# Group-normalisation statistics: two-operand steps on VectorE or on GpSimd

## The chip, the cores and the metric

The kernel runs on one core of one Trainium2 chip. The number that counts is the device time of one execution in microseconds (us). Before the change it is 6019.81 us, the median of three runs from 6017.21 to 6021.95. A profile of one execution, with a span of 6018.0 us, stands behind every other number here. The engines are called by the profile's names: PE is TensorE (matmuls), PEld its weight loads, DVE is VectorE, ACT is ScalarE, POOL is GpSimd, SP is the queue that issues transfers.

## The reference

Two layers on an input of 16 images, 56 x 56 pixels, 384 channels, in float32. Each layer normalises by groups and adds its result to its input.

```python
def _gn(v, G=32, eps=1e-5):                      # 32 groups of 12 channels, statistics per image
    g = v.reshape(B_, H_, W_, G, C_ // G)
    m = jnp.mean(g, axis=(1, 2, 4), keepdims=True)
    s = jnp.var(g, axis=(1, 2, 4), keepdims=True)
    return ((g - m) / jnp.sqrt(s + eps)).reshape(v.shape)

# layer 0: attention over 3x3 neighbours, three groups of channels with dilations 1, 2, 3
x = x + _L0_conv_ref(_gn(x), L0_conv_w_qkv, L0_conv_w_proj, L0_conv_b_proj)
# layer 1: depthwise 3x3 convolution with the signs of the weights
x = x + _L1_conv_ref(_gn(x), L1_conv_w)
```

So there are 32 group normalisations in all, two for each image. Each needs the whole image before it can give a mean and an inverse deviation, and everything behind it in its layer needs those.

## The kernel before

Channels lie on the partitions (three tiles of 128). An image is worked on in seven chunks of eight rows (448 pixels). Three stages are planned side by side: stage A turns the input round and gathers statistics of the first normalisation, stage B is the attention, stage C the convolution. Every piece of work is filed under a time slice, nine slices to a chunk, and the slices of different chunks and stages lie over each other:

```python
def at(when, order, piece):
    pieces.setdefault((when, order), []).append(piece)
...
SOFTMAX, SCORE, STATISTICS, CONVOLVE, WEIGH, QUERY, QKV, PROJECT, STAGE_A, STAGE_C, NORM, LOADS = range(12)
STEP = 9
for m in range(N):                 # N = 16 images x 7 chunks
    plan_a(m, STEP * (m - 9))
    plan_b(m, STEP * m)
    plan_c(m, STEP * (m + 10))
for key in sorted(pieces):
    for piece in pieces[key]:
        piece()
```

The recorded pieces are then put into an order for each engine by a scheduler; each engine executes its own row in that order. The heavy work of a chunk, cut to what is spoken of later:

```python
# score(i): query times keys, nine times a chunk
nc.vector.tensor_tensor(t..., q3, k3, ALU.mult)                       # L452, q3 in PSUM, k3 in SBUF
# ... then matmuls of t with sel add up the heads: ps (L437)

# softmax_2, softmax_3
nc.vector.tensor_tensor(by_neighbour(weights), by_neighbour(weights), over_neighbours(sm), ALU.mult)   # L485
nc.scalar.copy(term[0], e8)
nc.gpsimd.tensor_tensor(r8, e8, term[0], ALU.subtract)                # rest, L495
nc.scalar.copy(term[1], r8)
nc.gpsimd.tensor_tensor(term[2], r8, term[1], ALU.subtract)           # e, L497

# weigh(i): weights spread by a matmul (pb_a, L515), times values, summed; nine times a chunk
nc.vector.tensor_tensor(w..., pb[...], three(kv[1][g][m % V_SLOTS], DIL[g], ky), ALU.mult)   # L521, pb in PSUM
...
nc.gpsimd.tensor_tensor(w0, w0, w, ALU.add)                           # L529
if ky == 2:
    nc.gpsimd.tensor_tensor(y, w0[:, 0], w0[:, 1], ALU.add)           # L532
    nc.gpsimd.tensor_tensor(y, y, w0[:, 2], ALU.add)                  # L533
```

The statistics themselves are five pieces for each normalisation. Sums over the 12 channels of a group, and the way back from groups to channels, go through matmuls with 0/1 matrices (`gsel`, `gselT`); the inverse root is found by three Newton steps from an integer guess:

```python
def group_norm(stats, done):
    def channels():                                   # slice 0
        ... nc.vector.bn_aggr(ch[:, j, :], ...)       # mean and variance of each channel
    def mean():                                       # slice 1
        ... matmuls pm                                # L289
        nc.vector.tensor_scalar_mul(pair[:, 2:3], pm[:GN_G, 0:1], 1.0 / GN_CH)        # L292
    def deviation():                                  # slice 2
        ... matmuls pb                                # L299
        nc.vector.tensor_sub(dev, ch[:, :, 0], pb[:, :NG])                            # L301
        nc.vector.tensor_mul(dev, dev, dev)                                           # L302
        nc.vector.tensor_add(dev, dev, ch[:, :, 1])                                   # L303
    def invert():                                     # slice 3
        ... matmuls pv                                # L309
        nc.vector.tensor_scalar(v, pv[:GN_G, 0:1], 1.0 / GN_CH, 1e-5, ...)            # L312
        nc.vector.tensor_single_scalar(ri, v.bitcast(I32), 1, op=ALU.arith_shift_right)   # L315
        nc.vector.tensor_scalar(ri, ri, -1, RSQRT_BITS, op0=ALU.mult, op1=ALU.add)    # L316
        for step in range(3):
            nc.vector.scalar_tensor_tensor(t, r, v, r, op0=ALU.mult, op1=ALU.mult)    # L318
            nc.vector.tensor_scalar(t, t, -0.5, 1.5, op0=ALU.mult, op1=ALU.add)       # L319
            nc.vector.tensor_mul(pair[:, 1:2] if step == 2 else r, r, t)              # L320
        nc.vector.scalar_tensor_tensor(pair[:, 0:1], pair[:, 2:3], -1.0, pair[:, 1:2], ...)   # L321
    def spread_out():                                 # slice 4
        ... matmuls pp                                # L328
        nc.vector.tensor_copy(mr..., pp[:, : 2 * NG]) # L332
        done(mr)
    return channels, mean, deviation, invert, spread_out
```

`dev` has 128 partitions and three columns, everything from `v` on 32 partitions and one column. ScalarE normalises later with `mr` (bias and scale of `Identity`: L398 for the first layer, L624 and L666 for the second).

Of the kernel before, what the change touches and what calls it, by code (L numbers as in the profile page):

```python
# [8 lines left out]
F32 = mybir.dt.float32  # L9
# [3 lines left out]
ALU = mybir.AluOpType  # L13
# [7 lines left out]
NG = 3  # L21
# [4 lines left out]
GN_CH = 12  # L26
GN_G = 32
# [8 lines left out]
def dilated_attention_then_binary_conv(  # L36
# [28 lines left out]
    nc = tc.nc  # L65
# [10 lines left out]
    def place(p):  # L76

        g, o = divmod(p, NTAP)
        return NG * o + g
# [27 lines left out]
    for p in range(NG * NTAP):  # L107
        v = place(p)
# [126 lines left out]
    st_p = ctx.enter_context(tc.tile_pool(name="st_p", bufs=2))  # L235
# [3 lines left out]
    for which, slots in enumerate((K_SLOTS, V_SLOTS)):  # L239
        kv.append([])  # L240
        for g, d in enumerate(DIL):
            kv[which].append([])
            for s in range(slots):
                t = const.tile([P, ROWS + 2 * d, W + 2 * d], F32, name=f"{'kv'[which]}_{g}_{s}")
# [11 lines left out]
    for s in range(2):  # L256
        t = const.tile([P, ROWS + 2, W + 2], F32, name=f"zg_{s}")
# [17 lines left out]

    def group_norm(stats, done):

        had = {}

        def channels():  # L280
            had["ch"] = ch = st_p.tile([P, NG, 2], F32, tag="ch", name="ch")
            for j in range(NG):
                nc.vector.bn_aggr(ch[:, j, :], stats[:, j].rearrange("p c s -> p (c s)"))

        def mean():
            had["pair"] = pair = st_p.tile([GN_G, 3], F32, tag="pair", name="pair")
            pm = ps_mt.tile([P, 512], F32, tag="mt", name="pm")
            for j in range(NG):
                nc.tensor.matmul(  # L289
                    pm[:GN_G, 0:1], gsel[:, j], had["ch"][:, j, 0:1], start=(j == 0), stop=(j == NG - 1)  # L290
                )
            nc.vector.tensor_scalar_mul(pair[:, 2:3], pm[:GN_G, 0:1], 1.0 / GN_CH)  # L292

        def deviation():

            ch = had["ch"]
            pb = ps_mt.tile([P, 512], F32, tag="mt", name="pb")
            for j in range(NG):
                nc.tensor.matmul(pb[:, j : j + 1], gselT[:, j], had["pair"][:, 2:3], start=True, stop=True)  # L299
            had["dev"] = dev = st_p.tile([P, NG], F32, tag="dev", name="dev")  # L300
            nc.vector.tensor_sub(dev, ch[:, :, 0], pb[:, :NG])  # L301
            nc.vector.tensor_mul(dev, dev, dev)  # L302
            nc.vector.tensor_add(dev, dev, ch[:, :, 1])  # L303

        def invert():
            dev, pair = had["dev"], had["pair"]
            pv = ps_mt.tile([P, 512], F32, tag="mt", name="pv")
            for j in range(NG):
                nc.tensor.matmul(pv[:GN_G, 0:1], gsel[:, j], dev[:, j : j + 1], start=(j == 0), stop=(j == NG - 1))  # L309
            var = st_p.tile([GN_G, 3], F32, tag="var", name="var")  # L310
            v, r, t = var[:, 0:1], var[:, 1:2], var[:, 2:3]
            nc.vector.tensor_scalar(v, pv[:GN_G, 0:1], 1.0 / GN_CH, 1e-5, op0=ALU.mult, op1=ALU.add)  # L312

            ri = r.bitcast(I32)
            nc.vector.tensor_single_scalar(ri, v.bitcast(I32), 1, op=ALU.arith_shift_right)  # L315
            nc.vector.tensor_scalar(ri, ri, -1, RSQRT_BITS, op0=ALU.mult, op1=ALU.add)  # L316
            for step in range(3):
                nc.vector.scalar_tensor_tensor(t, r, v, r, op0=ALU.mult, op1=ALU.mult)  # L318
                nc.vector.tensor_scalar(t, t, -0.5, 1.5, op0=ALU.mult, op1=ALU.add)  # L319
                nc.vector.tensor_mul(pair[:, 1:2] if step == 2 else r, r, t)  # L320
            nc.vector.scalar_tensor_tensor(  # L321
                pair[:, 0:1], pair[:, 2:3], -1.0, pair[:, 1:2], op0=ALU.mult, op1=ALU.mult
            )

        def spread_out():
            pp = ps_mt.tile([P, 512], F32, tag="mt", name="pp")
            for j in range(NG):
                nc.tensor.matmul(  # L328
                    pp[:, 2 * j : 2 * j + 2], gselT[:, j], had["pair"][:, 0:2], start=True, stop=True
                )  # L330
            mr = st_p.tile([P, NG, 2], F32, tag="mr", name="mr", bufs=4)
            nc.vector.tensor_copy(mr.rearrange("p j s -> p (j s)"), pp[:, : 2 * NG])  # L332
            done(mr)

        return channels, mean, deviation, invert, spread_out

    def chunk_of(dram, c):
        return dram.rearrange("(j p) n -> p j n", p=P)[:, :, c * PX : (c + 1) * PX]
# [3 lines left out]
    def at(when, order, piece):  # L342

        pieces.setdefault((when, order), []).append(piece)
# [5 lines left out]
    def plan_a(m, t0):  # L350

        b, c = divmod(m, NCH)
        had = {}

        def load():
            if c == 0:
                stats0[b] = st_p.tile([P, NG, NCH, 6], F32, tag="stats0", name="stats0")
                xd[b] = dr_p.tile([C, H * W], F32, tag="xd", name="xd")
            had["xin"] = xin = xin_p.tile([SUB, NSUB, C], F32, tag="xin", name="xin")
            nc.sync.dma_start(xin, xf[b, c * PX : (c + 1) * PX, :].rearrange("(s p) c -> p s c", p=SUB))  # L360

        def turn(j):
            pt = ps_mt.tile([P, 512], F32, tag="mt", name="pt_x")
            for s in range(NSUB):
                nc.tensor.transpose(
                    pt[:, s * SUB : (s + 1) * SUB], had["xin"][:, s, j * P : (j + 1) * P], ident[:SUB, :SUB]
                )
            xa = xa_p.tile([P, PX], F32, tag="xa", name="xa")
            nc.scalar.copy(xa, pt[:, :PX])
            nc.vector.bn_stats(stats0[b][:, j, c, :], xa)  # L370
            nc.sync.dma_start(xd[b][j * P : (j + 1) * P, c * PX : (c + 1) * PX], xa)

        steps = {}

        def norm(k):
            if k == 0:
                steps["of"] = group_norm(stats0.pop(b), lambda mr: mr0.update({b: mr}))
            steps["of"][k]()

        at(t0 - 3, LOADS, load)  # L380
        for j in range(NG):
            at(t0 + 2 * j, STAGE_A, lambda j=j: turn(j))
        if c == NCH - 1:
            for k in range(5):
                at(t0 + 5 + k, STATISTICS, lambda k=k: norm(k))

    def plan_b(m, t0):

        b, c = divmod(m, NCH)
        had = {}  # L390
# [176 lines left out]
        def norm(k):  # L567
            if k == 0:
                steps["of"] = group_norm(stats1.pop(b), for_convolution)
            steps["of"][k]()  # L570
# [18 lines left out]
        for j in range(NG):  # L589
            at(t0 + 23 + j, PROJECT, lambda j=j: out_project(j))  # L590
        if c == NCH - 1:
            for k in range(5):
                at(t0 + 26 + k, STATISTICS, lambda k=k: norm(k))

    def plan_c(m, t0):
# [121 lines left out]
    for m in range(N):  # L717
# [3 lines that stand above are left out]
# [31 lines left out]
```

## Time and profile before

| engine | busy us | share of the span |
|---|---|---|
| TensorE (PE) | 5493.3 | 91% |
| VectorE (DVE) | 4382.1 | 73% |
| GpSimd (POOL) | 4191.8 | 70% |
| ScalarE (ACT) | 2616.6 | 43% |

A profile gives for every instruction its start and its length, and, from the semaphores, who ended the idle time before it. In a list of waits, "PE ps L437 <- DVE var L319" says that TensorE's instruction on line 437, which writes the tile `ps`, started when VectorE's on line 319, which writes `var`, had ended. A group's line gives how often the instruction runs, and its mean time or its shortest, median and longest. The heaviest groups of VectorE are the products of lines 521 (1556.5 us) and 452 (1543.5 us), those of GpSimd the additions of line 529 (2046.8 us) and, in the convolution, of line 681 (680.6 us). All of them are 128 x 1344 elements. Shares of busy time are averages over the whole span; which engine holds up the others can differ from stretch to stretch, so windows and timelines are read as well.

### The profile page before, as it was taken

Reading aid. Unit: us, or ns where it says so; the run is one execution under the profiler, and the core shown is the slowest. Engines: PE = TensorE matmul, PEld = TensorE weight load, DVE = VectorE, ACT = ScalarE, POOL = GpSimd, SP = SyncE. Lnnn points to the kernel's source line nnn. Section 1 sums busy time; section 2 is a strip of 40 time slices with the busy share of each in tenths; the row PEclk is TensorE's granted clock in tenths of the full one; section 3 lists DMA queues with packets and bytes.
Section 4 is the critical chain, followed back from the end, with each engine's and each line's share of the span. In section 5 each row is a group of like instructions: output and inputs, shape, how many; then the busy total and the mean of one; then the engine's idle time right before and its main releaser. Section 6 shows DMA issues by size and latency. Waiting matters only on the chain. (4 is left out here: it accounts for less than half of the span.)

```text
span 6018.0 us, 79851 instructions
## 1 busy us (share of the span) xinstructions
PE 5493.3 (91%) x28693; PEld 2517.5 (42%) x28693; DVE 4382.1 (73%) x4501; ACT 2616.6 (43%) x4714; POOL 4191.8 (70%) x2596
## 2 busy tenths in 40 slices
PE   5998999999999999999999999999999999999955
PEld 3443444444444444444444444444444444444421
DVE  3777777777777777777777778777777777777740
ACT  2223444544444444444544444444444444444435
POOL 1556677777777777777776777777777876777874
PEclk9998999999999999999999999999999999999975
DMA  4322444544445444444544444454444544433434
GB/s 148 100 90 89 123 134 135 145 134 131 136 130 146 135 132 134 135 130 134 145 139 128 132 132 139 128 146 135 129 136 132 147 135 131 134 118 105 115 99 119
DMA packets 629587, 776.73 MB, mean 129 GB/s; under 512 B 177091, under 2 KB 618950, under 8 KB 629190
## 3 DMA queue, kind: packets, MB, share of 16 engines
q1 hardware_dynamic: 624016, 771.01, 44.4%
q8 instruction: 227, 3.72, 0.3%
q14 instruction: 170, 1.39, 0.1%
q10 hardware_dynamic: 5174, 0.61, 0.1%
HBM read 468.47 MB, written 231.21 MB: 116 GB/s over the span
## 5 line engine op out<-in xcount | busy, mean ns | idle before, releaser
L529 POOL TENSOR_TENSOR w<-w 128x1344 f32<-128x1344 f32 x672 | 2046.8, 3046 | 789.7 <-DVE w L521 701.3
L521 DVE TENSOR_TENSOR w<-pb_a,v 128x1344 f32<-128x1344 f32 x1008 | 1556.5, 1544 | 350.1 <-PE pb_a L515 318.4
L452 DVE TENSOR_TENSOR t<-pq,k 128x1344 f32<-128x1344 f32 x1008 | 1543.5, 1548 | 239.6 <-PE pq L402 237.3
L402 PE MATMUL pkv<-xn,wqkvT 128*128 128x448 f32 x4032 | 1686.9, 569 | 0.0
L402 PEld LDWEIGHTS pkv<-xn,wqkvT 128*128 128x128 f32 x4032 | 771.3, 199 | 773.5 <-issue 708.3
L681 POOL TENSOR_TENSOR m<-m 128x1344 f32<-128x1344 f32 x224 | 680.6, 3039 | 296.9 <-ACT m L675 292.0
L402 PE MATMUL pq<-xn,wqkvT 128*128 128x448 f32 x2016 | 866.2, 564 | 0.0
L437 PE MATMUL ps<-t,sel 128*32 128x448 f32 x6048 | 766.8, 562 | 103.8 <-DVE var L319 62.6
L547 PE MATMUL po<-y,wprojT 128*128 128x448 f32 x2016 | 829.7, 548 | 23.5 <-POOL y L533 23.5
L675 ACT ACTIVATE m<-zg,ktap 128x448 f32<-128x448 f32 x1008 | 591.2, 660 | 426.8 <-POOL m L681 419.9
L641 PE MATMUL pc<-z,kdiag 96*32 96x440 f32 (+1 forms) x5376 | 575.0, 563 | 78.2 <-ACT z L624 42.4
L624 ACT ACTIVATE z<-z,mrz 96x448 f32<-96x448 f32 x896 | 627.5, 760 | 2.4 <-DMA mrz<-mr 2.3
L412 ACT COPY v<-pkv 128x448 f32<-128x448 f32 x336 | 177.9, 529 | 1030.1 <-PE pkv L402 1030.0
L550 DVE SCALAR_TENSOR_TENSOR xr<-po,bias,xr 128x448 f32<-128x448 f32 x336 | 228.6, 680 | 444.9 <-PE po L547 444.8
L547 PEld LDWEIGHTS po<-y,wprojT 128*128 128x128 f32 x2016 | 375.0, 191 | 380.9 <-issue 345.3
L402 PEld LDWEIGHTS pq<-xn,wqkvT 128*128 128x128 f32 x2016 | 357.7, 192 | 360.8 <-issue 360.8
L515 PE MATMUL pb_a<-aT,spread 24*128 24x448 bf16 x3024 | 386.7, 366 | 114.9 <-DVE w L521 110.5
L648 DVE TENSOR_TENSOR x<-pc,x 128x448 f32<-128x448 f32 x224 | 139.6, 623 | 368.8 <-PE pc L641 368.2
L533 POOL TENSOR_TENSOR y<-y,w 128x448 f32<-128x448 f32 x336 | 385.1, 1146 | 19.4
L532 POOL TENSOR_TENSOR y<-w 128x448 f32<-128x448 f32 x336 | 386.7, 1151 | 16.9
L515 PEld LDWEIGHTS <-spread 24*128 24x128 bf16 x3024 | 107.8, 92 | 604.3 <-issue 560.2
L398 ACT ACTIVATE xn<-xn,mr 128x448 f32<-128x448 f32 x336 | 234.5, 753 | 288.7 <-DMA xn<-xd 162.2
(111 smaller groups left out, 4869.6 us busy)
## 6 DMA issues: line engine op xcount, KB each, us to landing
z<-x1d SPq DMA_DIRECT2D x608, 224.0 KB, 3.8
xin<-in_x_dram SPq DMA_DIRECT2D x112, 672.0 KB, 6.4
xd<-xa SPq DMA_DIRECT2D x336, 224.0 KB, 2.2
xn<-xd SPq DMA_DIRECT2D x112, 672.0 KB, 4.4
xr<-xd SPq DMA_DIRECT2D x112, 672.0 KB, 4.1
x1d<-xr SPq DMA_DIRECT2D x112, 672.0 KB, 3.2
out_dram<-osb SPq DMA_DIRECT2D x448, 168.0 KB, 2.3
x<-x1d SPq DMA_DIRECT2D x112, 448.0 KB, 6.9
```

The source lines that it names most:

```text
L402: nc.tensor.matmul(dst[:, :PX], wqkvT[:, cc, o0 : o0 + P], had["xn"][:, cc, :], start=(cc == 0), stop=(cc == NG - 1))
L437: return nc.tensor.matmul(had["ps"][32 * j : 32 * j + 32, :PX], sel[:, s0 : s0 + 32], tk, start=(i == 0), stop=(p + NQ >= NG * NTAP),)
L452: nc.vector.tensor_tensor(t.rearrange("p k (r w) -> p k r w", w=W), q3, k3, ALU.mult)
L515: return nc.tensor.matmul(pb[:, kx, :PX], spread[rows_of, v % 2, :], had[f"a{v // 8}"][rows_of, :], start=True, stop=True)
L521: nc.vector.tensor_tensor(w.rearrange("p k (r w) -> p k r w", w=W), pb[:, :, :PX].rearrange("p k (r w) -> p k r w", w=W), three(kv[1][g][m ...
L529: nc.gpsimd.tensor_tensor(w0, w0, w, ALU.add)
L532: nc.gpsimd.tensor_tensor(y, w0[:, 0], w0[:, 1], ALU.add)
L547: nc.tensor.matmul(po[:, :PX], wprojT[:, g, j * P : (j + 1) * P], had[f"y{g}"], start=(g == 0), stop=(g == NG - 1))
L624: nc.scalar.activation(z[:, q], z[:, q], AF.Identity, bias=mrz[:, j, q, 0:1], scale=mrz[:, j, q, 1:2])
L641: return nc.tensor.matmul(pcr[q * HD : (q + 1) * HD, :, lo:hi], kdiag[:, kx, j * NQ + q, :], rows(z[:, q])[:, :, lo + kx - 1 : hi + kx - 1 ...
L675: nc.scalar.activation(rows(t[:, kx]), zp[:, ky : ky + ROWS, kx : kx + W], AF.Copy, scale=ktap[:, o : o + 1])
L681: nc.gpsimd.tensor_tensor(had["m"], had["m"], t, ALU.add)
```

## The change

Every step of the statistics whose two tensor operands both lie in SBUF goes from VectorE to GpSimd. [...] the steps that read a matmul's result stay on VectorE. The mean is kept with its sign turned, so that the deviation is an addition and the last product needs no extra factor. The fused product of three operands becomes two products. The piece `invert` is cut in two, `variance` (matmul and integer guess, VectorE) and `invert` (Newton steps, GpSimd), so there are six pieces in six slices instead of five in five. It is meant to keep these small steps out of VectorE's row.

```diff
-            nc.vector.tensor_scalar_mul(pair[:, 2:3], pm[:GN_G, 0:1], 1.0 / GN_CH)
+            nc.vector.tensor_scalar_mul(pair[:, 2:3], pm[:GN_G, 0:1], -1.0 / GN_CH)
...
-            nc.vector.tensor_sub(dev, ch[:, :, 0], pb[:, :NG])
-            nc.vector.tensor_mul(dev, dev, dev)
-            nc.vector.tensor_add(dev, dev, ch[:, :, 1])
+            nc.vector.tensor_tensor(dev, pb[:, :NG], ch[:, :, 0], ALU.add)
+            nc.gpsimd.tensor_tensor(dev, dev, dev, ALU.mult)
+            nc.gpsimd.tensor_tensor(dev, dev, ch[:, :, 1], ALU.add)
 
-        def invert():
+        def variance():
...              (matmuls pv, v and the integer guess as before, on VectorE)
+        def invert():
             for step in range(3):
-                nc.vector.scalar_tensor_tensor(t, r, v, r, op0=ALU.mult, op1=ALU.mult)
-                nc.vector.tensor_scalar(t, t, -0.5, 1.5, op0=ALU.mult, op1=ALU.add)
-                nc.vector.tensor_mul(pair[:, 1:2] if step == 2 else r, r, t)
-            nc.vector.scalar_tensor_tensor(
-                pair[:, 0:1], pair[:, 2:3], -1.0, pair[:, 1:2], op0=ALU.mult, op1=ALU.mult
-            )
+                nc.gpsimd.tensor_tensor(t, r, r, ALU.mult)
+                nc.gpsimd.tensor_tensor(t, t, v, ALU.mult)
+                nc.gpsimd.tensor_scalar(t, t, -0.5, 1.5, op0=ALU.mult, op1=ALU.add)
+                nc.gpsimd.tensor_tensor(pair[:, 1:2] if step == 2 else r, r, t, ALU.mult)
+            nc.gpsimd.tensor_tensor(pair[:, 0:1], pair[:, 2:3], pair[:, 1:2], ALU.mult)
...
-        return channels, mean, deviation, invert, spread_out
+        return channels, mean, deviation, variance, invert, spread_out
...              (for both layers)
-            for k in range(5):
+            for k in range(6):
```

In the changed file the lines move by a few numbers: the pair of additions on `dev` is L305 and L306, the Newton steps L326 to L329, the last product L330, `pp` L335, `mr` L339.

More of the change, by code (lines that the diff above doesn't have):

```diff
@@ L300, in deviation @@
             had["dev"] = dev = st_p.tile([P, NG], F32, tag="dev", name="dev")
-            nc.vector.tensor_sub(dev, ch[:, :, 0], pb[:, :NG])
-            nc.vector.tensor_mul(dev, dev, dev)
-            nc.vector.tensor_add(dev, dev, ch[:, :, 1])
-        def invert():
-            dev, pair = had["dev"], had["pair"]
+            nc.vector.tensor_tensor(dev, pb[:, :NG], ch[:, :, 0], ALU.add)
+            nc.gpsimd.tensor_tensor(dev, dev, dev, ALU.mult)
+            nc.gpsimd.tensor_tensor(dev, dev, ch[:, :, 1], ALU.add)
+        def variance():
+            dev = had["dev"]
             pv = ps_mt.tile([P, 512], F32, tag="mt", name="pv")
@@ L309, in invert @@
                 nc.tensor.matmul(pv[:GN_G, 0:1], gsel[:, j], dev[:, j : j + 1], start=(j == 0), stop=(j == NG - 1))
-            var = st_p.tile([GN_G, 3], F32, tag="var", name="var")
-            v, r, t = var[:, 0:1], var[:, 1:2], var[:, 2:3]
+            had["var"] = var = st_p.tile([GN_G, 3], F32, tag="var", name="var")
+            v, r = var[:, 0:1], var[:, 1:2]
             nc.vector.tensor_scalar(v, pv[:GN_G, 0:1], 1.0 / GN_CH, 1e-5, op0=ALU.mult, op1=ALU.add)
@@ L316, in invert @@
             nc.vector.tensor_scalar(ri, ri, -1, RSQRT_BITS, op0=ALU.mult, op1=ALU.add)
+        def invert():
+            var, pair = had["var"], had["pair"]
+            v, r, t = var[:, 0:1], var[:, 1:2], var[:, 2:3]
             for step in range(3):
[L318 to L321, printed above, removed]
-                pair[:, 0:1], pair[:, 2:3], -1.0, pair[:, 1:2], op0=ALU.mult, op1=ALU.mult
-            )
+                nc.gpsimd.tensor_tensor(t, r, r, ALU.mult)
[3 more added lines that the diff above has]
+            nc.gpsimd.tensor_tensor(pair[:, 0:1], pair[:, 2:3], pair[:, 1:2], ALU.mult)
         def spread_out():
@@ L591, in plan_b @@
         if c == NCH - 1:
-            for k in range(5):
+            for k in range(6):
                 at(t0 + 26 + k, STATISTICS, lambda k=k: norm(k))
```

## The prediction

> **What bounds the kernel now.** I read four views in this order: the busy times of the page, a table of windows with one window per chunk of eight image rows, the list of waits, and then the timelines of VectorE, GpSimd and TensorE through one group normalisation. The page first:
>
> ```profile
> PE 5493.3 (91%) x28693; PEld 2517.5 (42%) x28693; DVE 4382.1 (73%) x4501; ACT 2616.6 (43%) x4714; POOL 4191.8 (70%) x2596
> ```
>
> TensorE leads, with 525 us idle in the span. Cutting the span at the softmax copy of each chunk (L469) shows where those 525 us lie. The windows below are an undisturbed chunk, one that ends a normalisation of `x` (call it A, first layer), another undisturbed one, and one with a normalisation of `x1` (call it B, second layer). Columns: window, length, busy time and instruction count of each engine, granted clock, DMA share, GB/s.
>
> ```profile
> core 0: us, PE busy (x) PEld busy (x) DVE busy (x) ACT busy (x) POOL busy (x), PEclk, DMA share, GB/s
> 2049.31:2096.37 47.06, 46.87 (x258) 21.99 (x258) 37.81 (x40) 21.18 (x40) 37.29 (x23) 1.00 0.51 149
> 2096.37:2158.89 62.52, 51.57 (x265) 24.07 (x266) 44.26 (x52) 25.10 (x45) 37.24 (x27) 0.89 0.38 108
> 2158.89:2204.88 45.99, 45.95 (x249) 20.89 (x247) 35.71 (x34) 23.25 (x44) 36.63 (x23) 1.00 0.50 144
> 2298.77:2357.09 58.32, 51.22 (x274) 24.20 (x273) 44.98 (x54) 18.59 (x37) 35.22 (x23) 0.94 0.42 117
> ```
>
> The reader is to see that undisturbed chunks (46 to 47 us) are TensorE from end to end, and nothing done to VectorE can shorten them. Against 47.0 us, A costs 62.5 - 47.0 = 15.5 us more and B 58.3 - 47.0 = 11.3 us, and TensorE is idle for 62.52 - 51.57 = 11.0 and 58.32 - 51.22 = 7.1 us of that; the rest is a lower clock and the statistics' own matmuls. Each image has one A and one B, 26.8 us together. With 16 images, of which the first A and the last B lie in the ramps at the ends, 15 x 26.8 = 402 us is the most that any change to the statistics can bring.
>
> Who holds TensorE up, from the list of waits (total us, times, longest):
>
> ```profile
> PE pp L328 <- DVE pair L321: 68.9, 15, 5.2
> PE ps L437 <- DVE var L319: 62.6, 16, 4.1
> ```
>
> Sixteen times about 4 us, fifteen times about 5 us: once for each image and kind. And why VectorE is late, from the instructions that write `var` (ns min/median/max):
>
> ```profile
> L318 DVE SCALAR_TENSOR_TENSOR var<-var x96: 196/206/3067, 92.8 to 5843.8; 32x1 f32<-32x1 f32 x96
> L319 DVE TENSOR_SCALAR var<-var x96: 123/141/143, 93.0 to 5844.1; 32x1 f32<-32x1 f32 x96
> L320 DVE TENSOR_TENSOR var<-var x64: 135/1023/2969, 93.2 to 5843.6; 32x1 f32<-32x1 f32 x64
> ```
>
> One value per partition takes 135 ns at best and 3 us at worst, but only where both operands are tensors in SBUF. L319 has one and never leaves 143 ns. The timelines of the A in the second window show what the 3 us are (start, length; VectorE, then GpSimd, then TensorE):
>
> ```profile
> 2099.97 2.97 DVE L320 TENSOR_TENSOR var<-var 32x1 f32<-32x1 f32 x1
> 2102.87 1.54 DVE L452 TENSOR_TENSOR t<-pq,k 128x1344 f32<-128x1344 f32 x1
> 2105.04 1.53 DVE L521 TENSOR_TENSOR w<-pb_a,v 128x1344 f32<-128x1344 f32 x1
> 2107.09 2.67 DVE L318 SCALAR_TENSOR_TENSOR var<-var 32x1 f32<-32x1 f32 x1
> 2109.68 1.54 DVE L452 TENSOR_TENSOR t<-pq,k 128x1344 f32<-128x1344 f32 x1
> ```
>
> ```profile
> 2099.69 0.24 POOL L419 MEMSET k<- 128x186 f32 x1
> 2099.90 3.02 POOL L529 TENSOR_TENSOR w<-w 128x1344 f32<-128x1344 f32 x1
> ...
> 2106.72 3.03 POOL L529 TENSOR_TENSOR w<-w 128x1344 f32<-128x1344 f32 x1 [2.11 <-DVE var L320]
> ```
>
> ```profile
> 2096.54 0.35 PE L309 MATMUL pv<-dev,gsel 128*32 128x1 f32 x6 [0.23 <-DVE dev L303]
> ...
> 2106.63 0.56 PE L515 MATMUL pb_a<-aT,spread 24*128 24x448 bf16 x3 [5.82 <-DVE w L521]
> 2111.28 1.72 PE L437 MATMUL ps<-t,sel 128*32 128x448 f32 x8 [4.09 <-DVE var L319]
> ```
>
> L320 ends when the GpSimd addition that began at 2099.90 ends, L318 when the one from 2106.72 ends. The big products behind them (L452, L521) start late and TensorE waits for those. L452 and L521 themselves run beside the additions at an unchanged 1.54 us: one operand of theirs is in PSUM.
>
> **What the Trainium skill says.** "SBUF — State Buffer", section "Who interferes with whom": a VectorE instruction with two SBUF inputs needs the read port that GpSimd reads through, the port is held for a whole instruction, and the later one waits in full; with one SBUF input there is no such conflict. The three rows above agree: 2.97 and 2.67 us behind additions of 3.02 and 3.03. "GPSIMD Engine Reference", section 4.1, makes GpSimd about half as fast on two inputs. The trace agrees on big tiles (448 columns: 1146 ns on GpSimd, 623 for L648 on VectorE), which says little for 32x1. "Perfetto Trace Analysis", section "GPSIMD Engine Instruction", advises spacing rather than durations there; I use both below. "TensorE: Matmul & The Clock Gate", Part 1, puts the matmul clock at half after about 3.4 us of idleness, until a busy stretch of that order has passed. The 0.89 and 0.94 of the table agree, beside 1.00.
>
> **The change part by part.** (1) It removes from VectorE the two squares-and-adds of `dev` (L302, L303: 26.9 + 22.9 us) and all of the inversion's loop and last product (L318 77.4, L319 13.0, L320 97.3 + 16.0, L321 4.5). That is 258 us over 32 normalisations, 8.1 us each, most of it lock. It is not simply subtracted: it counts only where VectorE holds up TensorE.
>
> (2) It adds 15 instructions to GpSimd per normalisation. GpSimd's additions take 3046 ns for 1344 columns and 1146 for 448, so 2.12 ns a column and 0.2 us fixed; a dependent one starts 0.08 us after the end before it (gaps from L532 to L533). So about 0.28 us each, an estimate, 0.6 us for the pair on `dev` and 13 x 0.28 = 3.6 us for the inversion in one row. VectorE unhindered needs 94.57 - 92.78 = 1.8 us for the same inversion at the first image, so the work itself gets slower.
>
> (3) It moves the matmuls. In the built order of the changed kernel `pp` comes one slice later. In A, 12 matmuls of `pkv`, 4 of `pt_x`, 3 of `pt_o` now stand ahead of it; in B, two `pkv` projections and the weights' transposes.
>
> Now A, worked through by these durations from 2092.8 us. GpSimd's queue ahead of `dev` is the one before, a row of additions from 2092.28 that ends with the memset at 2099.93. So `dev` is ready at about 2100.5 where VectorE had it at 2096.5. TensorE reaches `pv` at 2096.3 and stalls **4.2 us: a new wait**. From there VectorE is no longer held: `var` by 2103.7, `t` behind `pq` at 2104 to 2105.5, its next `w` from 2106.1. GpSimd makes one more addition (to 2106.4) and then the inversion, to 2110.1. TensorE goes on with `pb_a`, `pq`, `pt_s`, `pb_a`, two `pkv`, transposes and scores, and reaches `pp` at about 2112 to 2114: no wait. So A keeps 4.2 us idle, some 1.7 us for a clock lowered in about half the cases (15.5 - 11.0 - 1.6 = 2.9 us now, where it is always lowered, so half of about 3), and 1.6 us of its own matmuls (`pv` 0.35, `pp` 1.28 in TensorE's timeline): 7.5 instead of 15.5, a gain of 8.0.
>
> B, from 1944.8 us: VectorE is busy without a gap up to 1973.3, and TensorE waits 0.90 at `pv`, 1.68 at `ps`, 3.71 at `pp`. There GpSimd is free when `dev` comes (its row ends at 1955.2, `dev` at 1955.9 instead of 1956.3), `rest` and `e` pass, the inversion runs from about 1959.0 to 1963. In TensorE's order `pp` comes only near 1971.7. About 0.4 us of idleness and 1.6 of its own matmuls stay: 2.0 instead of 11.3, a gain of 9.3.
>
> At the two ends the chain is exposed and gets longer: by 2 us at the first A, by perhaps 5 at the last B, where `dev` stands behind a memset that waits for ScalarE until 5843.5. Sum: 15 x (8.0 + 9.3) = 260, less 7, gives 253 us: 6020 - 253, rounded to 5770 us.
>
> **The rivals.** First, the wait only moves to GpSimd: its queue is strict, 70% busy in 3 us pieces, and A's 4.2 us are a case of it. If each small instruction costs 0.8 us instead of 0.28, the inversion takes 10 us, A's `pp` waits some 4 us again and the lower clock costs its whole 3; B, with 8 us of slack, hardly suffers. A then gains 2 instead of 8, and that leaves 15 x (2 + 9.3) = 170 less the ends, about 5860. For it: no two-input GpSimd instruction this small is in the trace. Against it: affine selects of four columns take 188 ns and memsets 0.1 to 0.25 us.
>
> Second, GpSimd becomes the bound: 15 x 0.28 x 32 = 134 us on 4192. Its 37 us per chunk of 47 refuse it; it would need several times the cost estimated.
>
> Third, all of A's and B's overhead goes except the matmuls: 15 x (26.8 - 3.2) = 354 us, 5670. It would need `dev` early in A, against the queue shown above.
>
> Fourth, VectorE has enough slack anyway and nothing changes: the two waits by name and the gapless timelines speak against it.
>
> **Range and chances.** 5690 at the low end (A's stall half as long, no lowered clock), 5890 at the high end (a little worse than the first rival). Two per cent is 120 us, under half of the gain worked out; I give 0.87 to faster, 0.10 to within 2%, 0.03 to slower, the last for a stall that I have not read in the new order.
>
> **What would show it.** Right: VectorE loses about 258 us of busy time; TensorE's idle time falls from 525 to about 300; its waits for L319 and L321 vanish; a wait for GpSimd's `dev` of about 4 us appears at `pv`, 15 times, in A only; A falls to about 54 us and B to about 49; undisturbed chunks stay at 46 to 47. Wrong: inversion steps spaced by far more than 0.3 us, a wait of `pp` for `pair`, or `w` and `t` still late on VectorE.

## The result and the profile after

The changed kernel takes 5817.89 us (median of four runs, 5804.47 to 5822.44) against 6018.51 us of the kernel before. The ratio is 0.9662, with a 95% interval from 0.9646 to 0.9679: some 200 us or 3.4% faster. The prediction was 5770 us, in a range from 5690 to 5890.

The page's busy times of the changed kernel (span 5820.6 us):

```profile
PE 5458.4 (94%) x28693; PEld 2494.8 (43%) x28693; DVE 4163.6 (72%) x4117; ACT 2616.1 (45%) x4714; POOL 4279.5 (74%) x3076
```

TensorE's idle time fell from 525 to 362 us. Its windows, cut at the softmax copy of each chunk: an undisturbed chunk, one with A, another undisturbed one, one with B, and the chunk after that B. Columns as before: window, length, busy time (and count) of PE, PEld, DVE, ACT, POOL, granted clock, DMA share, GB/s.

```profile
1983.31:2030.28 46.97, 46.78 (x258) 21.86 (x257) 36.90 (x40) 21.19 (x41) 37.22 (x23) 1.00 0.51 150
2030.28:2084.14 53.86, 49.68 (x265) 23.23 (x266) 37.63 (x40) 25.15 (x45) 39.31 (x42) 0.97 0.44 125
2084.14:2130.59 46.45, 46.09 (x249) 20.86 (x248) 36.28 (x34) 23.45 (x43) 37.21 (x23) 1.00 0.49 142
1881.65:1933.29 51.64, 49.08 (x271) 23.12 (x270) 36.31 (x41) 18.73 (x37) 37.86 (x38) 0.97 0.41 112
1933.29:1983.31 50.02, 47.94 (x250) 21.59 (x249) 36.93 (x35) 27.77 (x50) 39.68 (x21) 0.97 0.53 154
```

A lost 8 us of its length, B some 6, and in both VectorE's busy time is that of any other chunk (it was 44 to 45 us). The chunk after B is not an undisturbed one. What TensorE waits for now, from the list of waits (total us, times, longest):

```profile
PE pv L312 <- POOL dev L306: 84.6, 30, 4.1
PE pa L509 <- POOL e L504: 58.0, 40, 3.4
PE pb_a L522 <- DVE w L528: 13.6, 11, 3.5
```

and two lines of the kernel before, to compare with:

```profile
PE pb_a L515 <- DVE w L521: 110.5, 40, 5.8
PE pa L502 <- POOL e L497: 45.8, 33, 5.6
```

The waits for `var` and `pair` on VectorE, 63 and 69 us before, are no longer among the listed ones, and the longest of before, for VectorE's late product `w`, has fallen from 110.5 to 13.6 us. In their place stands GpSimd's `dev`. A's timeline shows why, GpSimd first, then TensorE (start, length):

```profile
2032.53 1.12 POOL L540 TENSOR_TENSOR y<-y,w 128x448 f32<-128x448 f32 x1
2033.60 0.24 POOL L426 MEMSET k<- 128x186 f32 x1
2033.81 0.18 POOL L305 TENSOR_TENSOR dev<-dev 128x3 f32<-128x3 f32 x1
2034.07 0.19 POOL L306 TENSOR_TENSOR dev<-dev,ch 128x3 f32<-128x3 f32 x1
2036.72 3.02 POOL L536 TENSOR_TENSOR w<-w 128x1344 f32<-128x1344 f32 x1 [2.45 <-DVE var L318]
2039.70 0.18 POOL L326 TENSOR_TENSOR var<-var 32x1 f32<-32x1 f32 x1
...
2042.87 0.18 POOL L330 TENSOR_TENSOR pair<-pair 32x1 f32<-32x1 f32 x1
```

```profile
2034.32 0.35 PE L312 MATMUL pv<-dev,gsel 128*32 128x1 f32 x6 [4.10 <-POOL dev L306]
2034.60 0.36 PE L522 MATMUL pb_a<-aT,spread 24*128 24x448 bf16 x3
2034.90 4.22 PE L409 MATMUL pq<-xn,wqkvT 128*128 128x448 f32 x6
...
2046.53 0.60 PE L335 MATMUL pp<-pair,gselT 32*128 32x2 f32 x4
```

`dev` takes 0.45 us of work and stands behind GpSimd's additions until 2033.81, with TensorE idle. After that wait six matmuls of `pq` take 4.22 us, where they took 2.52 before: the granted clock is 0.50 from 2035.36 to 2038.78 us. The Newton row runs from 2039.70 to 2043.05 and `pp` comes 3.5 us later, without a wait.

### The profile page after: what moved, and what is told of

Same layout as the page of the kernel before. It is cut to its first block, busy times and chain, and to the rows that moved or that the text cites. A ratio compares the mean times of both kernels' runs of the same rounds, so it can differ in the third digit from the quotient of the medians.

```text
span 5820.6 us, 79874 instructions
## 1 busy us (share of the span) xinstructions
PE 5458.4 (94%) x28693; PEld 2494.8 (43%) x28693; DVE 4163.6 (72%) x4117; ACT 2616.1 (45%) x4714; POOL 4279.5 (74%) x3076
## 5 line engine op out<-in xcount | busy, mean ns | idle before, releaser
L409 PE MATMUL pkv<-xn,wqkvT 128*128 128x448 f32 x4032 | 1634.1, 554 | 0.0
L409 PEld LDWEIGHTS pkv<-xn,wqkvT 128*128 128x128 f32 x4032 | 746.6, 192 | 763.8 <-issue 695.1
L409 PE MATMUL pq<-xn,wqkvT 128*128 128x448 f32 x2016 | 889.9, 578 | 0.0
L648 PE MATMUL pc<-z,kdiag 96*32 96x440 f32 (+1 forms) x5376 | 587.0, 572 | 80.7 <-ACT z L631 43.8
L409 PEld LDWEIGHTS pq<-xn,wqkvT 128*128 128x128 f32 x2016 | 370.0, 197 | 350.4 <-issue 350.3
L522 PE MATMUL pb_a<-aT,spread 24*128 24x448 bf16 x3024 | 389.1, 364 | 13.6 <-DVE w L528 13.6
L648 PEld LDWEIGHTS pc<-z,kdiag 96*32 96x32 f32 x5376 | 184.5, 114 | 413.3 <-issue 322.6
L419 ACT COPY k<-pkv 128x448 f32<-128x448 f32 x336 | 179.4, 534 | 345.4 <-PE pkv L409 340.8
```

The source lines that it names most:

```text
L409: nc.tensor.matmul(dst[:, :PX], wqkvT[:, cc, o0 : o0 + P], had["xn"][:, cc, :], start=(cc == 0), stop=(cc == NG - 1))
L522: return nc.tensor.matmul(pb[:, kx, :PX], spread[rows_of, v % 2, :], had[f"a{v // 8}"][rows_of, :], start=True, stop=True)
L648: return nc.tensor.matmul(pcr[q * HD : (q + 1) * HD, :, lo:hi], kdiag[:, kx, j * NQ + q, :], rows(z[:, q])[:, :, lo + kx - 1 : hi + kx - 1 ...
```

## The experiments

Times are medians of four runs (e6: eight). The three right-hand columns are lengths from the traces, each the mean over twelve images in the middle of the run. "dev" and "Newton" tell on which engine these steps run, and in which form.

| kernel | dev | Newton | slices | us | A | B | chunk after B |
|---|---|---|---|---|---|---|---|
| before | VectorE, two tensors | VectorE, two tensors | 5 | 6018 | 62.6 | 58.4 | 48.9 |
| changed | GpSimd | GpSimd | 6 | 5818 | 54.4 | 52.3 | 50.9 |
| e1 | VectorE, two tensors | GpSimd | 6 | 5679 | 48.5 | 48.8 | 50.0 |
| e2 | GpSimd | VectorE, two tensors | 6 | 5993 | 63.1 | 55.7 | 50.1 |
| e3 | VectorE, two tensors | VectorE, two tensors | 6 | 5945 | 58.9 | 57.4 | 48.9 |
| e4 | VectorE, one tensor | VectorE, one tensor | 6 | 5726 | 55.1 | 47.6 | 47.2 |
| e5 | VectorE, one tensor | GpSimd | 6 | 5622 | 48.3 | 47.7 | 47.2 |
| e8 | VectorE, one tensor | A GpSimd, B VectorE one tensor | 6 | 5629 | 48.4 | 47.5 | 47.2 |
| e9 | changed, plus nine products of two tensors on VectorE | | 6 | 5922 | 60.7 | 52.4 | 50.7 |
| e10 | changed, plus nine products of one tensor | | 6 | 5836 | 55.4 | 52.6 | 50.9 |
| e11 | GpSimd | GpSimd | 5 | 5874 | 59.1 | 55.1 | 45.3 |

An undisturbed chunk is 47 us on average in all of them (singly 45.4 to 49.4). e6 and e7 are not in the table: they rest on a control with a flaw, told below.

**e1: only the Newton steps on GpSimd.**

```diff
-            nc.gpsimd.tensor_tensor(dev, dev, dev, ALU.mult)
-            nc.gpsimd.tensor_tensor(dev, dev, ch[:, :, 1], ALU.add)
+            nc.vector.tensor_mul(dev, dev, dev)
+            nc.vector.tensor_add(dev, dev, ch[:, :, 1])
```

> The changed kernel (5818 us), but the square and the addition on dev go back to VectorE; only the Newton steps stay on GpSimd. Theory L (the port shared by VectorE and GpSimd is the cost, and the new wait at pv is the place of dev in GpSimd's row): the wait of 4.1 us at pv in A goes, the one of 1.3 to 2.4 us in B shrinks below 1 us, and VectorE gets back up to 1.6 us of waiting for the port per normalisation. 15 x (3 to 5) us less: 5740 to 5775 us. Rival S (what helps is the sixth slice, which puts more matmuls ahead of pp): the same as the changed kernel within 1%, 5800 to 5840. Rival V (only the number of VectorE instructions counts): slightly slower, 5825 to 5840.

Measured: 5679 us, ratio to the kernel before 0.9438 (0.9424 to 0.9452). It is 139 us faster than the changed kernel, more than any theory gave. The two steps wait for the port again (median 780 and 940 ns, from 150 unhindered), and still this is the better place: one of the change's two moves was a loss. A falls by 5.9 us, where the wait of 4.1 and the clock behind it were. B falls by 3.5, and here another thing came to light, in TensorE's timeline of a B:

```profile
1848.12 2.52 PE L409 MATMUL pq<-xn,wqkvT 128*128 128x448 f32 x6
1851.46 0.32 PE L312 MATMUL pv<-dev,gsel 128*32 128x1 f32 x6 [0.83 <-DVE dev L306]
```

and in the changed kernel's B:

```profile
1891.59 0.96 PE L444 MATMUL ps<-t,sel 128*32 128x448 f32 x8
1894.96 0.28 PE L312 MATMUL pv<-dev,gsel 128*32 128x1 f32 x4 [2.42 <-POOL dev L306]
```

With `dev` on VectorE the scheduler keeps `pq` ahead of `pv`, as in the kernel before; with `dev` on GpSimd it puts `pq` behind `pv`, and TensorE arrives at `pv` before `dev` is there. In B all thirteen kernels follow this: `pq` is ahead in each with `dev` on VectorE and behind in each with `dev` on GpSimd.

**e2: only dev on GpSimd.**

```diff
-                nc.gpsimd.tensor_tensor(t, r, r, ALU.mult)
-                nc.gpsimd.tensor_tensor(t, t, v, ALU.mult)
-                ... (tensor_scalar and the product with r, on GpSimd)
+                nc.vector.scalar_tensor_tensor(t, r, v, r, op0=ALU.mult, op1=ALU.mult)
+                ... (the same two on VectorE; the last product too)
```

> The changed kernel, but the Newton steps go back to VectorE, in the old fused form; only the two steps on dev stay on GpSimd. Theory L: the long waits of VectorE for the port (up to 3 us on each of several Newton steps) are back, and A keeps its wait at pv: most of the gain is lost, 5920 to 6000 us. Rival S: pp still stands a slice later, 5800 to 5850. Rival V: ten VectorE instructions back at 0.14 to 0.2 us, 1.6 us in 32 places, under 5870.

Measured: 5993 us, 0.9958 (0.9943 to 0.9973), the far end of theory L's range: nearly the whole gain is gone. TensorE waits both for GpSimd's `dev` (83 us in 30 waits) and for VectorE's late `t` (93 us in 44).

**e3: six slices, everything on VectorE.** The edits of e1 and e2 together.

> Six slices, mean kept negative, but every step on VectorE as in the kernel before. Theory L: VectorE waits for the port as before and is late with its big products; only the wait of TensorE at pp (69 us in the kernel before) can be covered by the matmuls now ahead of it. 5940 to 6000 us. Rival S: the whole gain is here, 5800 to 5850. Rival V: as before, 6020.

Measured: 5945 us, 0.9879 (0.9864 to 0.9893), as theory L gave it; rival S (the whole gain) and rival V (no gain) fall. So the sixth slice and the turned sign bring 73 us by themselves. The Newton steps then bring 266 us by going to GpSimd if `dev` is on VectorE (5945 to 5679), and 175 if it is not (5993 to 5818). `dev` costs 48 or 139 us by going.

**e4: everything on VectorE, with one tensor operand each.** The other operand is given as a per-partition scalar: one value for each partition, read from a column in SBUF.

```diff
+            for j in range(NG):
+                nc.vector.tensor_scalar(dev[:, j:j+1], dev[:, j:j+1], dev[:, j:j+1], ch[:, j, 1:2],
+                                        op0=ALU.mult, op1=ALU.add)
...
+                nc.vector.tensor_scalar(t, r, v, r, op0=ALU.mult, op1=ALU.mult)
+                nc.vector.tensor_scalar(t, t, -0.5, 1.5, op0=ALU.mult, op1=ALU.add)
+                nc.vector.tensor_scalar(pair[:, 1:2] if step == 2 else r, r, t, None, op0=ALU.mult)
...              (the last product in the same form)
```

> Six slices, nothing on GpSimd: every step on VectorE, but written with one tensor operand and the others as per-partition scalars (three column-wise multiply-adds on dev, ten on the 32 x 1 column). Theory L: no step needs the shared port, each lasts 0.13 to 0.21 us, nothing waits in GpSimd's row: A and B both fall to about 49 to 51 us, 15 x (4 + 3) us below the changed kernel, 5690 to 5740. Rival V: 16 instructions more on VectorE per normalisation than in the changed kernel, so no better than it, 5830 to 5900. Rival P (a scalar operand is read through the same port as a second tensor): like the six slices with the fused form, 5940 to 6000, with single steps of up to 3 us.

Measured: 5726 us, 0.9516 (0.95 to 0.9532). The instructions that write `var` (ns min/median/max):

```profile
L328 DVE TENSOR_SCALAR var<-var x96: 162/259/261, 94.4 to 5554.3; 32x1 f32<-32x1 f32 x96
L329 DVE TENSOR_SCALAR var<-var x96: 123/134/143, 94.7 to 5554.6; 32x1 f32<-32x1 f32 x96
L330 DVE TENSOR_SCALAR var<-var x64: 191/192/202, 94.9 to 5554.0; 32x1 f32<-32x1 f32 x64
```

The same arithmetic on the same engine, and the 3 us are gone: no step exceeds 261 ns. Rival P falls, and rival V with it. B is where theory L put it. A is not: it stays at 55 us, because TensorE waits 2.7 us for a `t` that stands behind the Newton steps and the softmax product of `ew` and `sm` (the exponentials times the inverse of their sums). That product still has two tensors in SBUF and took 2.23 us there, from 0.58 unhindered.

**e5 and e8: dev with one tensor on VectorE, Newton on GpSimd.** The edit of e1 with e4's form of `dev`; e8 has GpSimd's Newton steps for the first layer alone and e4's for the second.

> dev on VectorE in three column-wise multiply-adds with scalar operands (as in the one-operand kernel, 5726 us), Newton steps on GpSimd (as in the kernel with only those there, 5679 us). Theory Q: the 2.3 to 3.9 us that TensorE waits for e in the chunk after B come from the 13 steps in GpSimd's row, which the one-operand kernel does not have (no such wait there): then this kernel keeps that wait, gains only the 0.5 us of pv in B, and stands at 5665 to 5680. Theory W: that wait comes from VectorE having waited for the port at dev: then it goes, and the time is 5630 to 5650.

> A towards the best of both: dev in one-operand form on VectorE everywhere; the Newton steps on GpSimd for the first layer (A, 48.5 us in the kernel with only the Newton steps there) and on VectorE in one-operand form for the second (B, 47.6 us and 47.2 us for the chunk after it in the one-operand kernel). Theory: the two parts do not touch each other, so A stays at 48 to 49, B at 47.5 to 48.5 and the chunk after B at 47 to 48: 5610 to 5640 us. If GpSimd's row in A spoils something later in the image, or the scheduler's new order does, 5650 to 5690.

Measured: e5 5622 us, 0.9341 (0.9327 to 0.9355); e8 5629 us, 0.9355 (0.9339 to 0.937). They agree to 0.15%, so for B it does not matter where the Newton steps are. e5 is the fastest of all, 397 us below the kernel before. Its busy times and the three windows B, chunk after B, and A:

```profile
PE 5371.9 (96%) x28693; PEld 2465.0 (44%) x28693; DVE 4171.6 (74%) x4213; ACT 2621.8 (47%) x4714; POOL 4264.2 (76%) x3012
```

```profile
1824.75:1871.76 47.01, 46.70 (x269) 22.04 (x267) 35.84 (x42) 18.84 (x37) 41.31 (x38) 1.00 0.48 133
1871.76:1919.00 47.24, 47.10 (x254) 21.52 (x252) 36.76 (x36) 27.74 (x50) 35.71 (x20) 1.00 0.53 153
1965.74:2014.45 48.71, 48.45 (x264) 22.50 (x262) 38.76 (x40) 25.46 (x45) 39.66 (x40) 1.00 0.49 140
```

TensorE is idle for 0.1 to 0.3 us in each and its clock stays at 1.00. Of the two theories on the wait for `e` in the chunk after B, Q falls (e5 has the Newton steps in GpSimd's row and no such wait to speak of). W named the right result (5630 to 5650; e5 is a little faster still), but the row of GpSimd speaks for another cause. In the changed kernel's chunk after B:

```profile
1933.52 3.05 POOL L688 TENSOR_TENSOR m<-m 128x1344 f32<-128x1344 f32 x1 [1.97 <-ACT m L682]
1936.65 2.35 POOL L693 TENSOR_TENSOR m<-m 128x448 f32<-128x448 f32 x2
...
1949.11 1.16 POOL L502 TENSOR_TENSOR rest<-ew,e 112x512 f32<-112x512 f32 x1
1951.00 1.15 POOL L504 TENSOR_TENSOR e<-rest,e 112x512 bf16<-112x512 f32 x1 [0.73 <-ACT e L503]
```

and in e5's:

```profile
1862.03 3.06 POOL L690 TENSOR_TENSOR m<-m 128x1344 f32<-128x1344 f32 x1
1865.16 2.34 POOL L695 TENSOR_TENSOR m<-m 128x448 f32<-128x448 f32 x2
...
1885.90 1.16 POOL L504 TENSOR_TENSOR rest<-ew,e 112x512 f32<-112x512 f32 x1 [2.22 <-ACT e L503]
```

In e5 the scheduler has put the convolution's additions `m` some 10 us earlier (9.7 us ahead of the chunk's start instead of 0.2 us behind it), and GpSimd stands waiting when `rest` is due. In the changed kernel its row is full from `m` to `rest`, and TensorE waits for `e`. All thirteen kernels agree: where the additions stand 0.2 us behind the start (the nine others, the kernel before among them), TensorE waits for `e`, 1.9 to 2.7 us on average; where they stand earlier, in e4, e5, e8 (some 9.7 us ahead) and e11 (4 us ahead), it does not. No run moved these additions alone, so this is what the rows agree on and not a test.

**e6, e7, e9, e10: nine more products on VectorE.** In each the changed kernel, and after the integer guess

```diff
+            for _ in range(9):
+                nc.vector.tensor_mul(junk, v, r)                              # e6; e9 with v, v
+                nc.vector.tensor_scalar(junk, v, r, None, op0=ALU.mult)       # e7; e10 with v, v
```

> The changed kernel (5818 us) and nothing taken from it: nine more VectorE products of two SBUF columns (32 x 1) after the integer guess, into a tile that nobody reads. Theory L: some of them wait for the port behind GpSimd's additions, up to 3 us each, and delay the big products behind them; TensorE waits for t and w again: 15 x (3 to 8) us, 5860 to 5940. Rival V (only the count of VectorE instructions matters): the same as the next kernel, with nine one-operand products, within 0.3%.

> The changed kernel and nine more VectorE products with one tensor operand and one per-partition scalar, at the same place, into a tile that nobody reads. Theory L: none waits for the port, 9 x 0.19 us on an engine with slack: 5815 to 5845 us, each instruction at most 0.25 us. Rival V: as the kernel with two tensors.

Measured: e6 6001 us, 0.9971 (0.9961 to 0.9982); e7 5962 us, 0.9904 (0.988 to 0.9929). Both missed theory L's figures by far, e7 although none of its products took more than 203 ns. The fault lay in the control: the products read `r`, which GpSimd's first Newton step overwrites, so GpSimd had to wait for products scattered over VectorE's row, and `pp` for GpSimd. From e7's list of waits:

```profile
PE pp L338 <- POOL pair L333: 90.6, 18, 5.9
```

That is no cost of the products themselves, so the pair was run again reading `v` alone.

> The control again without its flaw: in the two kernels with nine more products GpSimd's write of r had to wait for the last of them, which read r. Here all nine read v alone, which nobody writes again. The changed kernel (5818 us) with nine more products of two SBUF tensors on VectorE. Theory L: some of them last up to 3 us behind GpSimd's additions, B (52.3 us) grows by some 3 us as it did with the flawed control, A (54.4 us) by 3 to 5: 5880 to 5940 us. Rival V: the same as the next kernel within 0.3%.

> The same nine products with one tensor and one per-partition scalar, both v. Theory L: each at most 0.25 us, B unchanged at 52 to 53, A at most 2 us longer: 5815 to 5850 us. Rival V: as the kernel with two tensors.

Measured: e9 5922 us, 0.9846 (0.983 to 0.9861); e10 5836 us, 0.9694 (0.9679 to 0.9709). The products of e9 and e10 (ns min/median/max):

```profile
L322 DVE TENSOR_TENSOR junk<-var x288: 130/148/2960, 93.7 to 5749.7; 32x1 f32<-32x1 f32 x144
```

```profile
L322 DVE TENSOR_SCALAR junk<-var x288: 184/194/204, 95.2 to 5661.8; 32x1 f32<-32x1 f32 x144
```

By the median the two-tensor form is even the shorter one; the few that wait for the port make it 86 us dearer. Nobody reads the results, so this is the delay of what stands behind them in VectorE's row. Rival V falls. Nine instructions that do not wait cost 18 us (0.3%), hardly outside the noise: the intervals of the two ratios touch at 0.9679. The growth lies in A (54.4 to 60.7 against 55.4); B, for which theory L gave some 3 us, did not grow in either.

**e11: the changed kernel in five slices.**

```diff
-        return channels, mean, deviation, variance, invert, spread_out
+        return channels, mean, deviation, lambda: (variance(), invert()), spread_out
...              (for both layers)
-            for k in range(6):
+            for k in range(5):
```

> The changed kernel with its pieces variance and invert called in one slice, so five slices as before. In the built order of A only pb_a, pq, pt_s and pb_a (about 4.2 us of matmuls) then stand between pv and pp; GpSimd has pair ready 8.5 us after pv. If the sixth slice is there to cover GpSimd's Newton row, pp waits about 4 us for pair in A and hardly in B (about 9 us of matmuls against 7), and the clock falls with it: 15 x (4 to 7), 5880 to 5925 us. If the sixth slice does nothing here: 5810 to 5830.

Measured: 5874 us, 0.9766 (0.9749 to 0.9783), 56 us slower than six slices. In A `pp` waits for `pair`:

```profile
PE pp L335 <- POOL pair L330: 44.9, 17, 4.5
```

A grows by 4.7 us as expected, though the wait itself is 2.4 us on average there and not 4. B and the chunk after it, taken together, fall by 2.8 us, and so the time ends just below the expected 5880 to 5925.

## Why the prediction was right, and where it was off

**The mechanism** was right and is shown: two SBUF tensors on VectorE wait behind GpSimd's additions, and what costs is the big product behind them (TensorE's waits for `w`, `t` and the statistics' own `var` and `pair`). e4 takes the wait away on the same engine, and e9 against e10 puts it back.

**A** was right in its sum and in its main terms: a gain of 8.0 us was expected, and A gained 62.6 - 54.4 = 8.2. The wait at `pv` was put at 4.2 us and is 4.1. A GpSimd step was put at 0.28 us and is spaced by 0.26; the Newton row was put at 3.6 us and takes 3.35. `pp` has no wait. Two smaller terms were off and cancel, which is luck. The clock was to be lowered in about half of the A's, for 1.7 us (half of the 2.9 named there would be 1.5); it is lowered in all twelve, which costs some 2.2 us (an estimate, as in B: half of TensorE's busy time in the stretches whose granted clock is 0.50). And the statistics' own matmuls were put at 1.6 us, where some 1.0 remains: the 1.28 us of `pp` had been read from a stretch of the old trace whose granted clock was 0.50.

**B** was off: a gain of 9.3 us was expected, and B gained 6.1, of which the chunk after it gives 2.0 back. The step that failed is "about 0.4 us of idleness" at `pv`, with no lowered clock behind it, and with it the sign that the wait for `dev` stands "in A only". It took the time at which TensorE reaches `pv` from the old trace, where `pq` stands ahead of `pv`. In the built order of the changed kernel `pq` stands behind it; TensorE arrives some 2.5 us sooner and waits 1.9 us on average (1.3 to 2.4). In seven of the twelve B's, those with 2.0 us or more, the clock falls soon after; so in the B shown above, whose wait ended at 1894.96 (columns as in the windows above; the granted clock is 0.50):

```profile
1895.42:1898.83 3.41, 3.41 (x24) 1.51 (x16) 0.36 (x3) 0.62 (x1) 2.43 (x6) 0.50 0.00 0
```

Over the twelve this costs 1.7 us on average; with 1.5 us more of waiting it makes up the 3.2 us that are missing. e1, where `pq` is ahead, has B at 48.8 us, the 49 that the prediction gave, at a clock of 1.00. The 2.0 us in the next chunk no step had foreseen. There `pa` starts 18.9 us after the chunk's start in both kernels, so `e` is no later; TensorE has less to do ahead of it and waits 2.67 us on average instead of 1.89, and the chunk's mean clock is 0.95 instead of 0.99, some 2.0 us by the same estimate.

**The sum**: 15 x (8.2 + 6.1 - 2.0) = 185 us of the 197 by which the two spans differ, against 260 in the prediction; the other 12 lie outside these windows. TensorE's idle time fell to 362 us and not to about 300. The ends cost less than the 7 us allowed. From the mean to `mr` the first A went from 6.9 to 8.5 us, the last B from 8.4 to 9.1; the memset ahead of the last `dev` was already done.

**VectorE's busy time** fell by 218 us instead of 258. The rows of neighbouring instructions overlap by some 0.07 us in this profile, so the removed rows (12 a normalisation) added up to some 27 us more than their share. Also the product of `ew` and `sm` now takes 1029 ns a time instead of 890, 15.5 us in all; that it meets GpSimd's additions more often is the likely reason.

**The rivals.** The first was half right. The wait did move to GpSimd, but to `dev` and not to the Newton row: two short steps in a queue of long ones cost 139 us (e1), while the 13 that had a slice to themselves delay no `pp`. The second, GpSimd as the bound, and the fourth, no change, fall: GpSimd is 74% busy, and the time fell by 3.4%. The third, "all of A's and B's overhead goes", is what e5 reaches with `dev` off GpSimd: 5622 us, where 5670 was given for it.

## What to carry to other kernels

Before moving a small step to another engine, ask where it will stand in that engine's queue and who waits for its result: a step whose result a busy engine needs at once is better kept where the queue is short, even at a worse price each (e1). Try first to take the cause of the wait away in place. Here a column as a per-partition scalar operand, instead of a second tensor, needed no move at all and, with the sixth slice, brought 292 of the 397 us that e5 reaches (e4). And when a prediction follows an engine through a changed program, read the order of every engine in the new program, not only of the ones that the change names.

## What the runs showed of the hardware

A per-partition scalar operand in SBUF did not bring the wait for the shared port that a second tensor brings: over 288 products each, the longest took 204 ns with one tensor and one scalar (e10) and 2960 ns with two tensors (e9). It has a small price: on a 32 x 1 column the median was 134 ns with two constants, 192 with one such scalar, 259 with two (e4).

A 32 x 1 step on GpSimd took 180 to 183 ns and the next dependent one began 0.08 us after its end, so one step each 0.26 us. On VectorE, at the first image of the kernel before, where nothing delays the steps, it was one each 0.20 us (nine steps from 92.78 to 94.57). For columns as small as these GpSimd was slower by about a third.

Waits of TensorE shorter than the 3.4 us that the prediction went by already lower its clock. In the twelve B's of the changed kernel, waits of 2.0 to 2.4 us at `pv` were followed by a granted clock of 0.50 in seven cases of seven, for 3.4 or 6.8 us, and waits of 1.3 to 1.4 us in none of five. In the chunk after B of the kernel before, waits of 1.9 us were followed by it in three cases of twelve.
